# A transformer block with routed experts on one core: the third pair of routed tiles is transposed from its first fetch of rows, ahead of the first outputs

## The chip, the cores and the metric

The kernel runs on one core of a Trainium2 chip. The metric is device time in microseconds of one execution; lower is better. All numbers are float32 unless a listing says otherwise.

## The reference, cut to what matters

Sixteen batches of 512 rows with 256 columns are normalised. To the input are added a linear attention and a two-level mixture of experts. In the latter each row has one hidden vector h of 512 that all experts share; two of eight experts, both of one group of four, multiply it with their own matrix, weighted by the router.

```python
xn = _layernorm(x, axis=-1)
# attention: q, k = elu(.)+1 of projections, kv = sum over rows of k v^T per head
out = (q @ kv) / max(q . sum(k), eps) @ Wo + bo
# mixture: shared part, and two routed experts for each row
shared = _swiglu(flat @ w_in.T) @ w_out.T
h = _swiglu(flat @ w1.T)
for e in range(NUM_EXPERTS):
    routed = routed + h * w_se[:, e:e + 1] @ w2[e].T
x = x + attention + shared + routed
```

## The kernel before, in words

The first part of the kernel loops over the 16 batches. For each it normalises, projects q and k, routes, and computes the hidden rows h (function `hidden_rows`, which stores them to a DRAM table `h_d`, columns 0 to 511). Function `gather` then sums the shared expert and the attention in PSUM, adds them to the residual `res`, and stores that with the two router weights to the same rows of `h_d` (columns 512 to 769). So a row of `h_d` holds all that the routed part needs: h, the base to add to, and two weights. The h columns of the last batch are in the table before `gather` of the last batch runs; the base columns of that batch only after it.

Function `order` sorts all 8192 rows by their pair of experts (twelve pairs are possible) into tiles of 128 rows, each tile with one pair. At least 67 tiles are worked on (`SURE`); more only if the counts ask for it. The lists `source` and `goal` tell which rows a tile takes and where its results go.

The second part loops over pairs of tiles (class `Tiles`, two tiles each; the last has one). Each pair goes through three steps:

- `rows()` (line 654): GpSimd issues one indirect DMA for each of the two tiles, which gathers 128 rows of `h_d` into one of four buffers, in turn `kk_all`, `qq_all`, `xn_all` and `hs_all`. These are buffers of the first part that are free by then; `hs_all` is free only when `gather` of the last batch has read it.
- `turn()` turns h into the stationary operand `hT`, in blocks of 32 by 32. ScalarE copies three of four quadrants of rows to other partitions (line 673, tile `hb`, twelve copies), VectorE transposes the first quadrant straight from the fetched rows (line 680, four instructions) and the others from `hb` (line 686, three instructions). `hT` has two buffers (tag xnT), `hb` two (tag blocks).
- `sums()` (lines 703 to 716): TensorE multiplies each tile with the matrices of its two experts (line 703, eight matmul instructions a tile), VectorE weights and adds the halves to the base (lines 710 and 713, tile `y`), and GpSimd stores the rows to the output with an indirect DMA (line 716).

The order of issue on each engine is the order of the program as the scheduler arranges it, unless a line asks for another (`tc.issue_after`). On GpSimd all fetches and all stores of the routed part are in one queue. `AHEAD` is 3: at the change of the two parts, the first three pairs are fetched before `gather` of the last batch, so that their h is at hand early; the first two are turned right after `gather`, VectorE's part behind the last two additions of line 535 (list `taken`). Then the fourth pair is fetched, and the first three are fetched once more, because their base columns may belong to the last batch:

```python
    tiles[AHEAD].rows()
    for w in tiles[:AHEAD]:
        w.rows()
```

In the loop that follows, the pair g+3 is fetched, the pair g+2 is turned and the pair g is summed. So before the change the third pair is turned in the loop's first pass, that is from the second fetch. Buffers of the fetched rows come round after four pairs, those of `hT` after two.

Of the kernel before, what the change touches and what calls it, by code (L numbers as in the profile page):

```python
# [12 lines left out]
ALU = mybir.AluOpType  # L13
# [8 lines left out]
def block_kernel(  # L22
# [29 lines left out]
    nc = tc.nc  # L52
    B, S, D = x.shape
# [23 lines left out]
    AHEAD = 3  # L77
# [21 lines left out]
    def load_x(b, pieces=1):  # L99
        xt = xp.tile([P, NT, D], FP, tag="x", name=f"x_{b}")  # L100
        n = NT // pieces
        for i in range(pieces):
            nc.sync.dma_start(
                out=xt[:, ts(i, n), :], in_=x[b, ts(i, n * P), :].rearrange("(t p) d -> p t d", p=P)
            )
        return xt
# [61 lines left out]
    def load_expert(i):  # L168
        W = HID // NQ
        for q in range(NQ):  # L170
            tc.keep_in_program_order(nc.sync.dma_start(
                out=w2_sb[ts(q, Q), :, ts(i, D)],
                in_=w2[ts(q, W), i // NL * EG + LINE[i % NL], :].rearrange("(c j) d -> j c d", j=Q),
            ))
# [57 lines left out]
    def turn(to, rows, tag, b, parts):  # L232

        blocks = work.tile([P, S // Q, KD * Q], FP, tag="blocks", name=f"{tag}_{b}")
        for q in range(NQ):
            nc.sync.dma_start(
                out=blocks[ts(q, Q)],
                in_=rows[:, ts(q, KD * Q)].rearrange("(n j) m -> j n m", j=Q),
            )

        def place():
            return nc.vector.transpose(  # L242
                to.rearrange("p c (n j) -> p n c j", j=Q),
                blocks.rearrange(f"p n {parts} -> p n c i", i=Q),
            )

        return place
# [205 lines left out]
    def key_sum(b, kk):  # L453

        k2 = one.tile([P, 2, D], FP, tag="k2", name=f"k2_{b}")
        nc.gpsimd.tensor_tensor(k2, kk[:, 0:2, :], kk[:, 2:4, :], ALU.add)  # L456
        nc.gpsimd.tensor_tensor(k2[:, 0, :], k2[:, 0, :], k2[:, 1, :], ALU.add)
        pks = ps_mm.tile([P, D], FP, tag="mm", name=f"pks_{b}")
        nc.tensor.matmul(pks, lhsT=ones, rhs=k2[:, 0, :], start=True, stop=True)  # L459
        ksb = work.tile([P, D], FP, tag="ksb", name=f"ksb_{b}")  # L460
        nc.vector.tensor_copy(ksb, pks)
        return ksb

    def summarize(b, xn, kk):

        pxk = ps_mm.tile([P, KD, D], FP, tag="mm", name=f"pxk_{b}")
        for c in range(KD):
            for t in range(NT):
                nc.tensor.matmul(  # L469
                    pxk[:, c, :], lhsT=xn[:, t, ts(c, P)], rhs=kk[:, t, :],  # L470
                    start=(t == 0), stop=(t == NT - 1),
                )
        xk = one.tile([P, KD, D], FP, tag="xk", name=f"xk_{b}")
        nc.scalar.copy(xk, pxk)
        return xk
# [166 lines left out]
    class Tiles:  # L642
# [17 lines left out]
        def turn(self, after=None):  # L660

            n, W = self.n, HID // NQ
            self.hT = work.tile([P, KH, 2 * P], FP, tag="xnT", name=f"hT_{self.tiles[0]}")
            to = self.hT.rearrange("p c (n a j) -> p n c a j", n=2, a=NQ)[:, 0:n]
            near = 1
            there = work.tile([P, NQ - near, 2, W], FP, tag="blocks", name=f"hb_{self.tiles[0]}")  # L670
            for a in range(near, NQ):
                for q in range(NQ):
                    nc.scalar.copy(  # L673
                        there[ts(q, Q), a - near, 0:n, :], self.hg[ts(a, Q), 0:n, ts(q, W)]
                    )
            wait = (lambda: tc.issue_after(after.ins)) if after else nullcontext
            for a in range(near):
                for q in range(NQ):
                    with wait():
                        nc.vector.transpose(  # L680
                            to[ts(q, Q), :, :, a, :],
                            self.hg[ts(a, Q), 0:n, ts(q, W)].rearrange("p n (c i) -> p n c i", i=Q),
                        )
            for a in range(near, NQ):
                with wait():
                    nc.vector.transpose(  # L686
                        to[:, :, :, a, :],
                        there[:, a - near, 0:n, :].rearrange("p n (c i) -> p n c i", i=Q),
                    )
            return self  # L690

        def sums(self):

            for j, i in enumerate(self.tiles):
                if i % TR == 0:
                    _, regs[:] = nc.values_load_multi_w_load_instructions(
                        self.where[i // TR : i // TR + 1, :], engines=[mybir.EngineType.PE],
                        min_val=0, max_val=(G * NL - 2) * D,
                        skip_runtime_bounds_check_because="a sum of steps up to one of the pairs, whatever the counts",
                    )  # L700
                py = ps_mm.tile([P, 2, D], FP, tag="mm", name=f"py_{i}")
                for f in range(KH):
                    nc.tensor.matmul(  # L703
                        py.rearrange("p j d -> p (j d)"), lhsT=self.hT[:, f, ts(j, P)],
                        rhs=w2_sb[:, f, bass.ds(regs[i % TR], 2 * D)],
                        start=(f == 0), stop=(f == KH - 1),
                    )
                base = self.hg[:, j, HID:ROW]
                y = work.tile([P, D], FP, tag="y", name=f"y_{i}", bufs=4)
                nc.vector.scalar_tensor_tensor(  # L710
                    y, py[:, 0, :], base[:, D : D + 1], base[:, 0:D], ALU.mult, ALU.add
                )
                nc.vector.scalar_tensor_tensor(  # L713
                    y, py[:, 1, :], base[:, D + 1 : D + 2], y, ALU.mult, ALU.add
                )
                stored = nc.gpsimd.indirect_dma_start(  # L716
                    out=out_rows,
                    out_offset=bass.IndirectOffsetOnAxis(ap=self.goal[:, i : i + 1], axis=0),
                    in_=y, in_offset=None, bounds_check=TT * P - 1, oob_is_err=False,
                )  # L720

                tc.declare_no_dep(stored.ins, group="out", reason="no two tiles write to the same row")
                tc.add_to_no_dep_group("out", stored.ins)

    def front(b, xnT):

        res = residual(b)
        qq, kk, lg = project(b, xnT)
        route(b, lg, res)
        return res, qq, kk  # L730
# [8 lines left out]
    for b in range(B):  # L739
        xn, xnT, _ = normed.pop(b)  # L740
        res, qq, kk = fronts.pop(b)
        if b + 1 < B:
            fronts[b + 1] = front(b + 1, normed[b + 1][1])
        else:

            nc.sync.dma_start(
                out=h_d[ts(b, S), HID:ROW].rearrange("(t p) h -> p t h", p=P), in_=res
            )
            *lists, filled = order()
            tiles = [Tiles(list(range(i, min(i + 2, SURE))), *lists) for i in range(0, SURE, 2)]  # L750
        xk = summarize(b, xn, kk)
        if b == 0:
            sums = key_sum(0, kk)
            queries[0] = attend(0, qq, sums)
        if b + 2 < B:
            normed[b + 2] = normalize(b + 2)
        if b + 3 < B:
            xs[b + 3] = load_x(b + 3)
        hidden_rows(b, xnT)
        ksb, (qT, turned) = sums, queries.pop(b)  # L760
        turned()
        if b + 1 < B:
            sums = key_sum(b + 1, fronts[b + 1][2])
            queries[b + 1] = attend(b + 1, fronts[b + 1][1], sums)
        hs = hidden(b, xnT)
        kvo = mix(b, xk, ksb)
        if b + 2 < B:
            normed[b + 2][2]()
        if b + 1 == B:
            for w in tiles[:AHEAD]:  # L770
                w.rows()
        taken = gather(b, res, qT, kvo, hs)
        if b + 1 == B:

            tiles[0].turn(taken[-2])
            tiles[1].turn(taken[-1])

        for e in waiting[: 2 if b + 1 < B else G * NL]:
            load_expert(e)
        waiting = waiting[2:]  # L780
# [8 lines left out]
    for g, w in enumerate(tiles):  # L789
        if 0 < g < len(tiles) - AHEAD:  # L790
            tiles[g + AHEAD].rows()
        if g + AHEAD - 1 < len(tiles):
            tiles[g + AHEAD - 1].turn()
        w.sums()

    def rest(i):
        if i < TILES:
# [44 lines left out]
```

## Time and profile before

| | |
|---|---|
| median of three runs | 1091.64 us (1086.5, 1091.64, 1130.06) |
| the profiled execution | 1087.99 us |
| its span | 1086.2 us |
| TensorE busy | 1055.5 us (97%) |
| VectorE busy | 660.9 us (61%) |
| ScalarE busy | 375.9 us (35%) |
| GpSimd busy | 243.9 us (22%) |
| mean granted TensorE clock | 0.993 |

The span is the time from the first to the last instruction that the profiler saw in one execution. A row of the profile's groups gives line, engine, operation, output and input, the count, then the busy time in us and the mean in ns, and after the second bar the idle time of the engine ahead of it and what ended that. In a timeline the columns are start, duration (both in us), engine, line, operation and count, and in brackets the idle time ahead and what ended it. The clock row shows the TensorE clock granted, in tenths of full speed.

### The profile page before, as it was taken

The page shows a single profiled execution, that of the slowest core. Times are in us where ns is not written, and L with a number is a line of the kernel's source. Part 1 is how long each engine was busy: PE and PEld are TensorE (multiplying, and loading weights), DVE is VectorE, ACT ScalarE, POOL GpSimd, SP SyncE. Part 2 cuts the span into 40 slices and gives each one's busy share as a digit, 9 for nine tenths or more (in the row PEclk, how much of TensorE's full clock was granted, in tenths as well). Part 3 has the DMA queues.
Part 4 walks back from the last instruction along what each step waited for, and adds up shares of the span by engine and source line. Part 5 has one row for each costly group of instructions (what it writes and reads, how often), then busy time and mean ns, then how long its engine had stood idle before and what let it go on. Part 6 is the DMA issues. An engine that isn't in the chain of part 4 may idle for free.

```text
span 1086.2 us, 11307 instructions
## 1 busy us (share of the span) xinstructions
PE 1055.5 (97%) x3404; PEld 627.5 (58%) x3404; DVE 660.9 (61%) x1744; ACT 375.9 (35%) x703; POOL 243.9 (22%) x313
## 2 busy tenths in 40 slices
PE   6999999999999999999999999999999699999996
PEld 5574747575666657574747575666646244444442
DVE  7947466564647474746556464647395466666663
ACT  3413232223223131313222232212013667777761
POOL 6102011020202020101101020202003555555552
PEclk9999999999999999999999999999999899999999
DMA  7243342433424243423131323221114544555540
GB/s 228 97 117 117 78 135 59 135 92 105 133 69 136 69 136 88 125 59 115 41 116 57 100 72 91 81 63 63 59 40 133 185 136 152 150 151 152 153 151 34
DMA packets 129054, 116.02 MB, mean 107 GB/s; under 512 B 72109, under 2 KB 113597, under 8 KB 128736
## 3 DMA queue, kind: packets, MB, share of 16 engines
q1 hardware_dynamic: 119120, 77.16, 23.7%
q0 software_dynamic: 9456, 37.59, 11.4%
q8 instruction: 29, 0.48, 0.2%
q10 hardware_dynamic: 416, 0.52, 0.1%
q14 instruction: 33, 0.27, 0.1%
HBM read 65.36 MB, written 50.27 MB: 106 GB/s over the span
## 4 chain that ended last, share of the span: by engine, by line
PE 94%; DVE 2%; DMA 1%; issue 1%; ACT 0%; POOL 0%; SPq 0%; POOLq 0%; DVEq 0%; ACTq 0%
PE py L703 21%; PE phr L424 20%; PE phs L443 20%; PE po L534 15%; PE pxk L469 5%; PE pk L312 5%; PE pq L323 5%; PE pm L499 2%; PE pvk L482 1%; PE pks L459 1%; DMA x<-in_x 0%; DMA xn_all<-h_d,source 0%; ACT hb L673 0%; DMA hs_all<-h_d,source 0%; PE pi L614 0%
## 5 line engine op out<-in xcount | busy, mean ns | idle before, releaser
L703 PE MATMUL py<-w_sb,hT 128*128 x536 | 233.5, 599 | 10.0 <-DVE hT L686 10.0
L443 PE MATMUL phs<-xnT,win_sb 128*128 128x512 f32 x512 | 223.6, 593 | 0.0
L424 PE MATMUL phr<-w_sb,xnT 128*128 128x512 f32 x512 | 222.8, 593 | 0.0
L703 PEld LDWEIGHTS py<-w_sb,hT 128*128 128x128 f32 x536 | 103.0, 193 | 140.0 <-issue 138.9
L424 PEld LDWEIGHTS phr<-w_sb,xnT 128*128 128x128 f32 x512 | 97.3, 190 | 114.5 <-issue 106.0
L443 PEld LDWEIGHTS phs<-xnT,win_sb 128*128 128x128 f32 x512 | 97.0, 190 | 113.0 <-issue 110.3
L292 POOL TENSOR_TENSOR res<-x,bo_sb 128x1024 f32<-128x1024 f32 x16 | 37.9, 2369 | 433.9 <-DMA h_d<-res 323.4
L534 PE MATMUL po<-wout_sb,hs_all 128*128 128x256 f32 x512 | 123.6, 380 | 0.0
L535 DVE TENSOR_TENSOR res<-po,res 128x256 f32<-128x256 f32 x64 | 27.2, 424 | 131.8 <-PE po L534 131.8
L534 PEld LDWEIGHTS po<-wout_sb,hs_all 128*128 128x128 f32 x512 | 96.3, 191 | 12.2
L450 DVE TENSOR_TENSOR hs_all<-phs,sa_hs 128x512 f32<-128x512 f32 x64 | 43.5, 680 | 90.7 <-PE phs L443 85.4
L449 ACT ACTIVATE sa_hs<-phs 128x512 f32<-128x512 f32 x64 | 38.2, 597 | 158.4 <-PE phs L443 153.3
L716 POOL DMA_INDIRECT out<-y,goal x67 | 67.6, 1009 | 88.4 <-DVE y L713 78.0
L301 ACT ACTIVATE km<-km 128x1024 f32<-128x1024 f32 x16 | 16.9, 1057 | 177.4 <-DVE km L300 177.4
L432 DVE TENSOR_TENSOR hr<-phr,sa_hr 128x512 f32<-128x512 f32 x64 | 43.8, 684 | 55.7 <-PE phr L424 32.8
L430 ACT ACTIVATE sa_hr<-phr 128x512 f32<-128x512 f32 x64 | 38.0, 597 | 99.2 <-PE phr L424 93.3
L534 PE MATMUL po<-kvo,qT 128*128 128x256 f32 x256 | 67.0, 384 | 0.0
L312 PE MATMUL pk<-wkr_sb,xnT 128*128 128x266 f32 x256 | 61.3, 393 | 2.0 <-DVE xnT L242 1.7
L469 PE MATMUL pxk<-kk_all,xn_all 128*128 128x256 f32 x256 | 58.0, 380 | 0.0
L323 PE MATMUL pq<-wq_sb,xnT 128*128 128x256 f32 x256 | 57.9, 379 | 0.0
L456 POOL TENSOR_TENSOR k<-kk_all 128x512 f32<-128x512 f32 x16 | 27.6, 1727 | 127.8 <-DVE sm L358 125.3
L312 PEld LDWEIGHTS pk<-wkr_sb,xnT 128*128 128x128 f32 x256 | 49.1, 193 | 11.3 <-DVE xnT L242 2.1
(148 smaller groups left out, 1261.5 us busy)
## 6 DMA issues: line engine op xcount, KB each, us to landing
h_d<-hr SPq DMA_DIRECT2D x64, 256.0 KB, 2.6
h_d<-res SPq DMA_DIRECT2D x64, 129.0 KB, 1.9
q_d<-qq_all SPq DMA_DIRECT2D x16, 512.0 KB, 2.8
qb<-q_d SPq DMA_DIRECT2D x64, 128.0 KB, 2.6
w_sb<-in_w SPq DMA_DIRECT2D x64, 128.0 KB, 3.5
x<-in_x SPq DMA_DIRECT2D x15, 512.0 KB, 4.3
xn_d<-xn_all SPq DMA_DIRECT2D x14, 512.0 KB, 3.0
xb<-xn_d SPq DMA_DIRECT2D x56, 128.0 KB, 3.3
```

The source lines that it names most:

```text
L312: nc.tensor.matmul(pk, lhsT=xnT[:, k, ts(t, P)], rhs=wkr_sb[:, k, :], start=(k == 0), stop=(k == KD - 1),)
L323: nc.tensor.matmul(pq[:, t, :], lhsT=xnT[:, k, ts(t2 + t, P)], rhs=wq_sb[:, k, :], start=(k == 0), stop=(k == KD - 1),)
L424: nc.tensor.matmul(ph, lhsT=xnT[:, k, ts(t, P)], rhs=w1_sb[:, k, ts(half, HID)], start=(k == 0), stop=(k == KD - 1),)
L430: nc.scalar.activation(sa, halves[0], AF.Silu)
L432: nc.vector.tensor_tensor(hr, halves[1], sa, ALU.mult)
L443: nc.tensor.matmul(ph, lhsT=win_sb[:, k, ts(half * KH + f, P)], rhs=xnT[:, k, :], start=(k == 0), stop=(k == KD - 1),)
L449: nc.scalar.activation(sa, halves[0], AF.Silu)
L450: nc.vector.tensor_tensor(h[:, f, :], halves[1], sa, ALU.mult)
L469: nc.tensor.matmul(pxk[:, c, :], lhsT=xn[:, t, ts(c, P)], rhs=kk[:, t, :], start=(t == 0), stop=(t == NT - 1),)
L534: nc.tensor.matmul(po, lhsT=a, rhs=w, start=(i == 0), stop=(i == len(parts) - 1))
L703: nc.tensor.matmul(py.rearrange("p j d -> p (j d)"), lhsT=self.hT[:, f, ts(j, P)], rhs=w2_sb[:, f, bass.ds(regs[i % TR], 2 * D)], start=(f ...
L716: stored = nc.gpsimd.indirect_dma_start(out=out_rows, out_offset=bass.IndirectOffsetOnAxis(ap=self.goal[:, i : i + 1], axis=0), in_=y, in_ ...
```

## The change

The third pair (`tiles[2]`) is turned where the first two are, after `gather` of the last batch and ahead of the second fetch, from the rows of its first fetch. `turn()` keeps its last transpose in `self.turned`. The first pass of the loop no longer turns a pair; the later passes turn the same pairs as before. In the first pass `sums()` is given that transpose, and VectorE's first addition of each of the two first tiles is issued only behind it.

```diff
             for a in range(near, NQ):
                 with wait():
-                    nc.vector.transpose(
+                    self.turned = nc.vector.transpose(
                         to[:, :, :, a, :],
                         there[:, a - near, 0:n, :].rearrange("p n (c i) -> p n c i", i=Q),
                     )
             return self
 
-        def sums(self):
+        def sums(self, after=None):
...
-                nc.vector.scalar_tensor_tensor(
-                    y, py[:, 0, :], base[:, D : D + 1], base[:, 0:D], ALU.mult, ALU.add
-                )
+                with tc.issue_after(after.ins) if after else nullcontext():
+                    nc.vector.scalar_tensor_tensor(
+                        y, py[:, 0, :], base[:, D : D + 1], base[:, 0:D], ALU.mult, ALU.add
+                    )
...
             tiles[0].turn(taken[-2])
-            tiles[1].turn(taken[-1])
+            for w in tiles[1:AHEAD]:
+                w.turn(taken[-1])
...
-        if g + AHEAD - 1 < len(tiles):
+        if 0 < g < len(tiles) - AHEAD + 1:
             tiles[g + AHEAD - 1].turn()
-        w.sums()
+
+        w.sums(tiles[AHEAD - 1].turned if g == 0 else None)
```

## The prediction

> **What bounds the kernel now.** I read the page first: the busy shares, the two rows of tenths for PE and its clock, and the row of the routed matmuls.
>
> ```profile
> span 1086.2 us, 11307 instructions
> PE 1055.5 (97%) x3404; PEld 627.5 (58%) x3404; DVE 660.9 (61%) x1744; ACT 375.9 (35%) x703; POOL 243.9 (22%) x313
> ...
> PEclk9999999999999999999999999999999899999999
> ...
> L703 PE MATMUL py<-w_sb,hT 128*128 x536 | 233.5, 599 | 10.0 <-DVE hT L686 10.0
> ```
>
> TensorE is busy for 97% of the span, so only its gaps can be won. One slice of its clock row shows 8 instead of 9, and the routed matmuls of line 703 waited 10.0 us for transposes of line 686. PE's waits say how that splits.
>
> ```profile
> PE py L703 <- DVE hT L686: 10.0, 2, 9.2
> PE pt L280 <- DVE xn_all L270: 8.5, 2, 8.2
> ```
>
> Two waits for hT, one of 9.2 us (the columns are total, times, longest); the second row belongs to the start of the program. PE's timeline places the long one: after 32 matmuls, which are two pairs of routed tiles (4 tiles of 8), and ahead of the third pair.
>
> ```profile
> 833.45 14.00 PE L703 MATMUL py<-w_sb,hT 128*128 x32 [0.75 <-DVE hT L686]
> 856.69 23.76 PE L703 MATMUL py<-w_sb,hT 128*128 x48 [9.24 <-DVE hT L686]
> ```
>
> Next the windows, first of the stretch itself (the columns are PE, PEld, DVE, ACT and POOL busy, then clock, DMA share and GB/s), then of line 703 alone, pair by pair.
>
> ```profile
> 847.45:856.69 9.24, 0.00 (x1) 0.03 (x1) 5.81 (x14) 5.40 (x14) 5.75 (x6) 0.76 0.74 227
> 856.69:862.69 6.00, 6.00 (x7) 2.50 (x8) 1.56 (x4) 5.80 (x15) 1.99 (x2) 0.51 0.35 111
> ```
>
> ```profile
> 833.45:840.30 6.85, 6.85 (x16) 3.15 (x17) 1.00 0.40 124
> 856.69:866.60 9.91, 9.91 (x17) 4.26 (x18) 0.70 0.25 81
> 866.60:873.47 6.87, 6.87 (x18) 3.05 (x17) 1.00 0.25 76
> ```
>
> The gap costs twice. The third pair runs at clock 0.51 for its first 6.0 us and takes 9.91 us where the others take 6.86. What it waited for is seen on three queues. GpSimd's:
>
> ```profile
> 827.74 0.95 POOL L654 DMA_INDIRECT xn_all<-h_d,source  x1 [0.30 <-issue]
> 837.16 0.95 POOL L654 DMA_INDIRECT hs_all<-h_d,source  x1 [8.47 <-PE py L703]
> ...
> 845.96 0.95 POOL L654 DMA_INDIRECT xn_all<-h_d,source  x1 [0.30 <-issue]
> 847.22 1.03 POOL L716 DMA_INDIRECT out<-y,goal  x1 [0.30 <-issue]
> ...
> 851.14 0.98 POOL L654 DMA_INDIRECT kk_all<-h_d,source  x1 [0.30 <-issue]
> ```
>
> ScalarE's:
>
> ```profile
> 832.36 4.97 ACT L673 COPY hb<-qq_all 32x256 f32<-32x256 f32 x12
> 851.10 4.97 ACT L673 COPY hb<-xn_all 32x256 f32<-32x256 f32 x12 [13.76 <-DMA xn_all<-h_d,source]
> ```
>
> VectorE's:
>
> ```profile
> 837.37 0.45 DVE L686 STREAM_TRANSPOSE hT<-hb 128x256 f32<-128x256 f32 x1 [1.18 <-ACT hb L673]
> 844.42 0.48 DVE L710 SCALAR_TENSOR_TENSOR y<-py,kk_all 128x256 f32<-128x256 f32 x1 [6.61 <-DMA kk_all<-h_d,source]
> ...
> 850.77 1.78 DVE L680 STREAM_TRANSPOSE hT<-xn_all 32x256 f32<-32x256 f32 x4 [2.82 <-DMA xn_all<-h_d,source]
> ...
> 856.10 0.45 DVE L686 STREAM_TRANSPOSE hT<-hb 128x256 f32<-128x256 f32 x1 [0.24 <-ACT hb L673]
> ```
>
> The third pair's rows lie in xn_all. They are fetched twice. The second round starts at 837.16, and its fetch into xn_all, the last of eight, landed at 850.75 (issued at 845.96, 4.8 us to landing). Only then did ScalarE, idle for 13.76 us, copy and VectorE transpose. Yet the first fetch of the same rows was issued by 827.74, takes at most 4.7 us, so lay there from 832.4 on, unused.
>
> [...] The trace agrees on the halving (0.51) but gives other times: it fell about 4.9 us after the last matmul and came back 6.0 us after the next. I use the 6.0 us. [...] here 0.95 us against 3.7 to 4.9 us to landing, so I count landings. [...]
>
> **The change, part by part.** No instruction is added or removed: 12 copies, 7 transposes and all DMAs stay. They are recorded earlier, and GpSimd keeps its order.
>
> *ScalarE's copies for pair 3.* They follow those of pair 2, which end at 837.33 (832.36 + 4.97): data there since 832.4, the buffer of pair 1's copies free since 833.4. They run 837.33 to 842.30, in idle time.
>
> *VectorE's seven transposes.* hT has two buffers, so the third waits for pair 1's matmuls: 833.45 + 6.86 = 840.3, with the drain 840.5. Four of 0.44 us (1.77), then three of line 686 (1.10): done at about 843.5, in the idle 6.61 us. PE needs it at 833.45 + 2 x 6.86 = 847.2: slack 3.7 us. The gap of 9.24 us goes, and the half-clock stretch with it: 9.91 - 6.86 = 3.05 us. Together 12.3 us.
>
> *The added wait.* Both first outputs of line 711 wait for the last transpose (843.5), but kk_all's second fetch lands at 844.4 anyway. Price nothing, cover 0.9 us. Behind them queue y of the first pair, GpSimd's stores and the fetches of pair 5 (kk_all).
>
> *GpSimd's new wait.* The second fetch into xn_all must now wait for the last read of the first one, ScalarE's at 842.30 and VectorE's at 842.3. Its slot is 844.70: nothing, cover 2.4 us. SP's queue is not touched: its last stores are out by 834.2.
>
> *What is late next.* Pair 4 (hs_all) landed by 842.8; copies 842.8 to 847.8, transposes from 847.9 (behind y of the third tile) to 850.8; needed at 847.2 + 6.86 = 854.0: no wait. Pair 5 is the next: its fetch keeps its slot at 851.14 and took 4.9 us, landing at 856.0. Before, nobody needed it then (its matmuls started at about 873.4). Now ScalarE starts 0.35 us later as at 851.10, copies until 861.4, one transpose of 0.45 us more, and PE starts 0.14 us after that: 862.0, while PE comes free at 854.0 + 6.86 = 860.9. A new wait of 1.1 us. Were the landing as quick as in the later stream (3.9 us), it would be 0.1; with another microsecond of congestion, 2.1. I take 1.1; all stay under the 4.9 us at which the clock fell. Pair 6: copies 861.4 to 866.4, transposed at 866.9, needed at 862.0 + 6.86 = 868.9. Pair 7: its second fetch waits for the store of y behind pair 5's transposes, 864.3, landing 868.3, ready at about 874.1 against 875.7. After that the slack grows to the steady stream's 4 us, and the tail of 10.0 us after the last matmul stays.
>
> Sum: 9.24 + 3.05 - 1.1 = 11.2 us. The profiled execution took 1087.99 us (its span 1086.2 and 1.8 around it): 1087.99 - 11.2 = 1076.8. The median of the runs shown, 1091.64, stands 3.7 above that execution, the lowest at 1086.5. I say 1077.0, on the profiled execution's footing; on the median's it would be 1080.4, inside the range.
>
> **The rivals.**
>
> *A, as worked out: 1077.0.*
>
> *B, the wait moves to pair 5.* Late fetches, busier than in the trace of before (0.88 DMA share between 840 and 850), arrive some 4 us later: a gap of 5 us, in which the clock falls too, 3 us more. Gain 12.3 - 8 = 4.3: 1083.7. For it: 1.1 us are missing already. Against: up to 851 the traffic and its order are the same.
>
> *C, the clock stays low though the gap is gone.* Then 9.24 - 1.1 = 8.1: 1079.9. Against: it was 1.00 in all windows without a gap.
>
> *D, slower.* The new waits form a loop of queues: GpSimd's xn_all fetch stands ahead of the first stores and the fetches of pair 5, and is held until the third pair was read. If it issues late by d past 844.70, pair 5 is late by 1.1 + d, and 3 us of low clock join in. The gain of 12.3 is used up at d = 8.2, when the third pair's reads end after 852.9. With d = 12 it is slower by 3.8: 1091.8. For it: every fetch is in one queue. Against: copies and transposes have all their data ten microseconds before.
>
> *E, the change doesn't do what it says.* If the transposes still hung on the second fetch, the outputs would wait with them: about 1088. Against: the compiled order has the xn_all copies wait on the DMA semaphores of the first fetch, and its second fetch wait on ScalarE.
>
> **How the numbers follow.** A 0.77, B 0.10, C 0.05, D 0.04, E 0.04. The range, 1073 to 1085.5, takes A's 1075.8 to 1077.9 for the unknown landing, B and C, and the 3.7 us between execution and median. Two per cent, about what a measurement of this kernel can tell from no change, is 22 us; all of hT's waiting and the slow stretch are 13. Faster by over 2%: 0.02; within: 0.95; slower: 0.03, D grown or a disturbed measurement.
>
> **What would show it.** In the profile after: PE's longest wait for hT at about 1 us ahead of pair 5; clock 1.00 throughout 840 to 870; ScalarE's copies from xn_all starting at 837.3 without idling; VectorE's first output still at about 844.4, ended by kk_all's DMA. The first output at 848 or later would speak for D, a gap over 4 us before pair 5 for B, a span above 1082 against A.

## The result, and the profile after

The changed kernel took 1077.47 us (median of 6 runs, 1075.93 to 1079.28), the kernel before 1089.85 us (median of 6, 1085.69 to 1130.06). The ratio is 0.9897, with a 95% interval of 0.9873 to 0.9921, so the gain of 1.0% is clear of the noise, though small, and it is where the prediction put it. The ratio leaves out the execution of 1130.06 us, which is 4% above the fastest of its kernel. The profiled execution took 1076.49 us.

One thing is needed to read the times of all kernels here. Four of the eleven profiles shown or summed up below, one of them of the changed kernel, have a further wait of TensorE of 3.6 to 4.5 us near the start (it begins at 18.55, 18.57 and 18.73 us in three of them). The changed kernel's third profile shows half clock with it, 0.50 from 21.4 to 28.2 us; in two others the 16 matmuls of line 312 behind it take 5.2 and 5.3 us, where the 16 ahead of it took 4.8 and 4.9. It is far from the change. In these four and in the kernel with 8 more copies the first routed matmul starts at 837.0 to 838.9 us, in the others at 832.3 to 833.5, so it costs about 5 us. Each run has one kept profile, so that this wait also explains why the times of one kernel spread over some 5 us is likely, but not shown. What compares kernels best is therefore the routed stretch of the profiles, from the first matmul of line 703 to the last.

The page of the changed kernel (its lines behind the changed one are numbered one higher, so line 710 is now 711 and line 716 is 717):

```profile
span 1074.8 us, 11307 instructions
PE 1052.6 (98%) x3404; PEld 624.7 (58%) x3404; DVE 661.1 (62%) x1744; ACT 375.9 (35%) x703; POOL 244.9 (23%) x313
...
PEclk9999999999999999999999999999999999999999
...
L703 PE MATMUL py<-w_sb,hT 128*128 x536 | 230.5, 592 | 2.0 <-DVE hT L686 2.0
```

The counts of instructions are those of before. The clock row has no 8 any more, the routed matmuls are 3.0 us shorter in sum (230.5 for 233.5), and their wait for hT is 2.0 us for 10.0. PE's timeline shows what is left:

```profile
832.61 27.73 PE L703 MATMUL py<-w_sb,hT 128*128 x64 [0.75 <-DVE hT L686]
861.64 28.56 PE L703 MATMUL py<-w_sb,hT 128*128 x66 [1.29 <-DVE hT L686]
```

Four pairs run through where two did, and a new wait of 1.29 us stands ahead of the fifth. The windows of line 703 for pair 3 and pair 5 (PE, PEld, clock, DMA share, GB/s) put both at full clock:

```profile
846.33:853.20 6.87, 6.87 (x17) 3.04 (x16) 1.00 0.74 254
861.64:868.50 6.86, 6.86 (x16) 3.12 (x17) 1.00 0.48 149
```

The three queues behind it. ScalarE's timeline:

```profile
836.46 4.97 ACT L673 COPY hb<-xn_all 32x256 f32<-32x256 f32 x12
...
856.05 4.97 ACT L673 COPY hb<-kk_all 32x256 f32<-32x256 f32 x12 [7.62 <-DMA kk_all<-h_d,source]
```

VectorE's:

```profile
839.78 1.78 DVE L680 STREAM_TRANSPOSE hT<-xn_all 32x256 f32<-32x256 f32 x4 [2.87 <-PE py L703]
841.60 1.10 DVE L686 STREAM_TRANSPOSE hT<-hb 128x256 f32<-128x256 f32 x3
844.57 0.48 DVE L711 SCALAR_TENSOR_TENSOR y<-py,kk_all 128x256 f32<-128x256 f32 x1 [1.87 <-DMA kk_all<-h_d,source]
...
861.05 0.45 DVE L686 STREAM_TRANSPOSE hT<-hb 128x256 f32<-128x256 f32 x1 [1.22 <-ACT hb L673]
```

GpSimd's:

```profile
845.01 0.94 POOL L654 DMA_INDIRECT xn_all<-h_d,source  x1 [0.30 <-issue]
...
847.51 1.04 POOL L717 DMA_INDIRECT out<-y,goal  x1 [0.30 <-DVE y L711]
...
851.45 0.98 POOL L654 DMA_INDIRECT kk_all<-h_d,source  x1 [0.30 <-issue]
```

ScalarE copies the third pair without idling, its transposes end at 842.7 (841.60 + 1.10), and VectorE's first output (the addition of line 711) comes 1.87 us after that, when kk_all's fetch has landed: so the transposes lie in what had been idle time. GpSimd's second fetch into xn_all did not wait for the new reader (0.30 us ahead of it, ended by nothing but issue). The fetch of pair 5, issued at 851.45, lands at 856.0; copies to 861.0, the last transpose to 861.5, PE at 861.64. That chain is the new wait.

The routed stretch lasted 833.45 to 1076.16, 242.7 us, in the kernel before, and 832.61 to 1064.46, 231.85 us, in the changed one: 10.86 us less. Removed were 9.24 (gap) and 3.05 (half clock), added 1.29: 11.0. Of the 11.4 us between the two spans, another 0.84 lies ahead of the stretch, at the start of the program, and is no work of the change; the tail grew by 0.3.

### The profile page after: what moved, and what is told of

Its sections match the earlier page's. It is cut to its first block, busy times and chain, and to the rows that moved or that the text cites. A ratio compares the mean times of both kernels' runs of the same rounds, so it can differ in the third digit from the quotient of the medians.

```text
span 1074.8 us, 11307 instructions
## 1 busy us (share of the span) xinstructions
PE 1052.6 (98%) x3404; PEld 624.7 (58%) x3404; DVE 661.1 (62%) x1744; ACT 375.9 (35%) x703; POOL 244.9 (23%) x313
## 3 DMA queue, kind: packets, MB, share of 16 engines
q0 software_dynamic: 9456, 37.59, 11.4%
## 4 chain that ended last, share of the span: by engine, by line
PE 91%; DVE 4%; DMA 2%; issue 1%; ACT 1%; POOL 1%; SPq 0%; POOLq 0%; ACTq 0%; DVEq 0%
PE phs L443 20%; PE py L703 20%; PE phr L424 19%; PE po L534 15%; PE pk L312 5%; PE pxk L469 5%; PE pq L323 5%; PE pm L499 1%; PE pvk L482 1%; DMA kk_all<-h_d,source 1%; PE pks L459 1%; ACT hb L673 1%; DMA xn_all<-h_d,source 0%; DMA x<-in_x 0%; DVE qm L300 0%
## 5 line engine op out<-in xcount | busy, mean ns | idle before, releaser
L703 PE MATMUL py<-w_sb,hT 128*128 x536 | 230.5, 592 | 2.0 <-DVE hT L686 2.0
```

Source lines behind the costliest of these rows:

```text
L703: nc.tensor.matmul(py.rearrange("p j d -> p (j d)"), lhsT=self.hT[:, f, ts(j, P)], rhs=w2_sb[:, f, bass.ds(regs[i % TR], 2 * D)], start=(f ...
```

## The experiments

A sum is used in all of them. Take the changed kernel's stretch without its wait: 231.85 - 1.29 = 230.55 us. To it are added a kernel's waits for hT within the stretch and half of the TensorE time under half clock (0.50 to 0.51 in the windows). The third column is that sum, the last is measured from the first to the last routed matmul of each profile.

| kernel | waits; work at half clock (us) | sum | measured |
|---|---|---|---|
| before | 9.24; 5.9 | 242.7 | 242.7 |
| before, gap filled with matmuls | 8.75 of filler, 1.90; none | 241.2 | 241.0 |
| changed | 1.29; none | 231.85 | 231.85 |
| changed, without the order on the outputs | 2.02, 0.17; none | 232.7 | 233.0 |
| changed, another round of fetches, first time | 5.98; 6.2 | 239.6 | 239.6 |
| the same, second time | 0.52; none | 231.1 | 231.2 |
| changed, second time | 6.06; 3.2 | 238.2 | 238.2 |
| changed, third time | 1.25; none | 231.8 | 231.8 |
| changed, fourth time | 0.52; none | 231.1 | 231.1 |
| changed, 8 more copies | 1.55; none | 232.1 | 232.1 |
| changed, 24 more copies | 5.79, 0.81; 3.1 | 238.7 | 238.9 |

Sum and measurement agree within 0.3 us. So nothing else moves in the stretch: a kernel's time there is its waits and its clock. The experiments were run on three occasions, each on another chip. To the first belong the filled gap, the kernel without the order, the other round of fetches for the first time and the changed kernel for the second; to the next the changed kernel for the third time and both kernels with more copies; to the last the other round for the second time and the changed kernel for the fourth.

### Is the slow third pair a result of the gap? The gap filled with matmuls

The kernel before, with ten matmuls of 512 columns (20 instructions) on a spare PSUM tile behind the second pair. They add work that nobody reads.

```diff
-                    nc.tensor.matmul(
+                    self.last = nc.tensor.matmul(
...
         w.sums()
+        if g == 1:
+            fill = ps_y.tile([P, 2 * D], FP, tag="py", name="fill")
+            for f in range(10):
+                with tc.issue_after(w.last.ins):
+                    nc.tensor.matmul(
+                        fill, lhsT=w2_sb[:, f % KH, 0:P], rhs=w2_sb[:, f % KH, 0 : 2 * D],
+                        start=True, stop=True,
+                    )
```

> The kernel before, with ten extra matmuls of 128x512 (20 instructions, about 8.6 us at 0.43 us each) on TensorE between the second and the third pair; their result is not used. Nothing else moves: the third pair still starts when its transposes are done, some 23.2 us after the first routed matmul. Theory (the slow stretch is a consequence of TensorE's idling): the clock stays at 1.00, the third pair takes 6.9 us instead of 9.9, and the time is 3 us below the kernel before, about 1086.8 against its 1089.85 median (1085.0 against its profiled 1087.99). Rival (the slow stretch belongs to the transfers and transposes of those microseconds): the third pair still takes 9.9 us and the time stays that of the kernel before.

Measured: 1085.92 us (median of 22) beside 1088.37 for the kernel before (30), ratio 0.9982, interval 0.9968 to 0.9996. PE's timeline and the window of pair 3 (all engines, then clock, DMA share and GB/s):

```profile
851.00 8.75 PE L799 MATMUL fill<-w_sb 128*128 128x512 f32 x20
861.64 38.86 PE L703 MATMUL py<-w_sb,hT 128*128 x90 [1.90 <-DVE hT L686]
```

```profile
861.64:868.50 6.86, 6.86 (x16) 3.12 (x17) 2.41 (x6) 6.62 (x17) 2.80 (x3) 1.00 0.34 112
```

With 1.90 us of idle time instead of 9.24 the third pair takes 6.86 us at clock 1.00, though its rows still come from the second fetch. The half-clock stretch was the gap's own second cost, and it goes with the gap; the rival in which it stays has nothing left. The gain in time, 0.18%, is 2.4 us between the medians; the profile gives the 3.05 of the stretch less 1.4 by which pair 3 was later on that occasion (8.75 + 1.90 against 9.24).

### What does the order on the outputs bring? The changed kernel without it

```diff
-        w.sums(tiles[AHEAD - 1].turned if g == 0 else None)
+        w.sums()
```

> The changed kernel without its ordering edge: the first output is not issued behind the third pair's transposes. On VectorE the first tile's two additions then stand in front of these transposes, the second tile's behind them; on GpSimd the first fetch of the fifth pair moves ahead of the second fetch into xn_all. Theory (VectorE serves in order, and an addition that waits for kk_all's second fetch holds the transposes): the transposes start after the first output at about 845.5, the third pair is ready at 848.4 instead of 842.7, TensorE waits 2.2 us ahead of it and about 0.6 us ahead of the fifth pair instead of 1.3; the time is 1.5 us above the changed kernel, about 1079. Rival (the edge is idle, the early fetch alone brings the gain): no wait ahead of the third pair, and the same time as the changed kernel, 1077.5.

Measured: 1079.55 us (median of 6), ratio 0.9908, interval 0.9886 to 0.9929. PE's timeline of pairs 1 to 5, and VectorE's at the first outputs:

```profile
837.04 14.00 PE L703 MATMUL py<-w_sb,hT 128*128 x32 [0.74 <-DVE hT L686]
853.07 13.97 PE L703 MATMUL py<-w_sb,hT 128*128 x32 [2.02 <-DVE hT L686]
867.21 33.28 PE L703 MATMUL py<-w_sb,hT 128*128 x77 [0.17 <-DVE hT L686]
```

```profile
849.10 0.48 DVE L711 SCALAR_TENSOR_TENSOR y<-py,kk_all 128x256 f32<-128x256 f32 x1 [7.54 <-DMA kk_all<-h_d,source]
...
850.02 1.77 DVE L680 STREAM_TRANSPOSE hT<-xn_all 32x256 f32<-32x256 f32 x4
```

The first output takes VectorE's place and waits 7.54 us for kk_all's second fetch; the transposes of pair 3, whose buffer of hT was free from 843.9 on (837.04 + 6.86), stand behind it and begin at 850.02. Yet it costs only 2.02 us, and pair 5's wait falls to 0.17. The fetch that pair 5 waits for last did not come earlier: it was issued at 856.84, 19.80 us after the first routed matmul, for 18.84 in the changed kernel. TensorE itself was 2 us later, so this wait hides in the one ahead of pair 3. Turning pair 3 from its first fetch thus brings nearly all of the gain. What the order on the outputs brings is less sure. Against the first profile of the changed kernel it is 2.02 + 0.17 - 1.29 = 0.9 us. But on the occasion of this run the changed kernel took 1082.83 us, longer in each of its six runs than this one in any of its six, which fits the wait of 6 us that its profile has there (the next experiment shows it). So no run shows that the kernel with the order is the faster one.

### Is pair 5's wait that of its fetch? Another second round, twice, and the changed kernel beside it

The second round fetches the first pair, then the fourth, then the second; the third pair's second fetch goes behind pair 5's fetches.

```diff
-                nc.gpsimd.indirect_dma_start(
+                self.got = nc.gpsimd.indirect_dma_start(
...
-    tiles[AHEAD].rows()
-    for w in tiles[:AHEAD]:
+    for w in (tiles[0], tiles[AHEAD], tiles[1]):
         w.rows()
...
+        if g == 1:
+            with tc.issue_after(tiles[g + AHEAD].got.ins):
+                tiles[AHEAD - 1].rows()
```

> The changed kernel with GpSimd's second round of fetches in another order: kk_all ahead of hs_all, and the second fetch into xn_all behind the two fetches of the fifth pair. The same fetches and bytes. Theory (the fifth pair's wait of 1.29 us comes from its place in GpSimd's queue): the first outputs come 2 us earlier, the fifth pair's second fetch is issued at about 849.0 instead of 851.45 and lands at about 853.4, its transposes are done at 859.2 where TensorE comes free at 860.2; the wait of 1.29 us goes and no other comes; the time is 1.2 us below the changed kernel, about 1076.2. Rival (the wait comes from crowded transfers, which take the longer the closer they follow each other): the fetch lands at 855 or later and the wait stays near 1 us.

> The changed kernel once more, beside the others on the same chip. All theories: 1077.5 within 1.5 us; TensorE waits about 1.3 us ahead of the fifth pair and not ahead of the third, and the clock is 1.00 through the routed stretch.

Measured: 1083.54 us (median of 9, 1081.51 to 1086.12), ratio 0.9947, interval 0.9928 to 0.9966, and for the changed kernel beside it 1082.83 (median of 6, 1081.84 to 1083.64), ratio 0.9942, interval 0.9923 to 0.9961. They are 7.3 and 5.3 us above what the theory gave. The reordered kernel, ScalarE's timeline, VectorE's and PE's at pair 5:

```profile
853.50 4.98 ACT L673 COPY hb<-kk_all 32x256 f32<-32x256 f32 x12 [2.83 <-DMA kk_all<-h_d,source]
```

```profile
862.93 1.78 DVE L680 STREAM_TRANSPOSE hT<-kk_all 32x256 f32<-32x256 f32 x4 [7.17 <-remote]
```

```profile
865.98 19.19 PE L703 MATMUL py<-w_sb,hT 128*128 x37 [5.99 <-DVE hT L686]
```

The fetch came some 3 us earlier, as wanted: it was issued at 848.87, ScalarE's wait for it ended at 853.5, not at 855 or later as with the crowded transfers of the rival, and copies were done at 858.5. But VectorE began its transposes at 862.93 only ("remote" stands for a wait whose end the profile could not put down to an instruction or a transfer). The changed kernel on that occasion, the same three engines:

```profile
856.64 5.00 ACT L673 COPY hb<-kk_all 32x256 f32<-32x256 f32 x12 [7.87 <-issue]
```

```profile
856.88 0.48 DVE L711 SCALAR_TENSOR_TENSOR y<-py,xn_all 128x256 f32<-128x256 f32 x1 [4.25 <-PE py L703]
...
863.29 1.78 DVE L680 STREAM_TRANSPOSE hT<-kk_all 32x256 f32<-32x256 f32 x4 [5.40 <-remote]
```

```profile
866.34 3.97 PE L703 MATMUL py<-w_sb,hT 128*128 x5 [6.06 <-DVE hT L686]
```

Here too the rows were in time. What was late, as far as the records go, is VectorE's start behind TensorE: this output's matmuls ended, by the records, at 849.98, and it began at 856.88; the buffer of hT that the transposes need was last read at 853.4, and they began at 863.29. The profile puts 4.25 us of the first delay down to TensorE, and 5.40 us of the second to nothing that it could name. TensorE meanwhile went on through pairs 3 and 4 without a pause, so a delay of 7 to 10 us between the two is what the records show. That TensorE's signals came late is the author's reading of it, and no run here shows the cause. The kernel without the order, on the same occasion, had no such wait (2.02 us was its longest). A wait of 6 us ahead of pair 5 let the clock fall (0.50 from 862.7 to 869.5), which is rival B's outcome by another way than B's.

Both were run once more on a later occasion.

> The reordered second round (kk_all's rows first, xn_all's second fetch behind those of pair 5) measured once more, because on the first occasion VectorE saw TensorE's signals late and pair 5 waited 6 us for that alone. Theory: the wait ahead of pair 5 is that of its fetch; with the fetch issued some 2.5 to 3 us earlier it is gone (below 0.4 us), and the time is 1 to 1.3 us below that of the changed kernel on the same occasion, near 1076. Rival: pair 5 is bound by VectorE's queue and TensorE's signals, not by its fetch; a wait of 1 us or more (up to 6) stays ahead of it and the time is that of the changed kernel or longer.

> The changed kernel beside the reordered one. Theory: 1077, with a wait of 1.2 to 1.5 us ahead of pair 5, ended by ScalarE's copies of kk_all, which wait for its fetch. Rival, where TensorE's signals are seen late again: a wait of 6 us ahead of pair 5 with kk_all already landed and copied, and 1082.

Measured: 1075.68 us (median of 6), ratio 0.989, interval 0.9872 to 0.9907, for the reordered kernel, and 1076.55 us (median of 5), ratio 0.9895, interval 0.988 to 0.991, for the changed one. PE's timelines, first of the reordered kernel, then of the changed one:

```profile
837.36 34.72 PE L703 MATMUL py<-w_sb,hT 128*128 x80 [0.75 <-DVE hT L686]
872.60 27.70 PE L703 MATMUL py<-w_sb,hT 128*128 x64 [0.52 <-DVE hT L686]
```

```profile
832.62 27.73 PE L703 MATMUL py<-w_sb,hT 128*128 x64 [0.74 <-DVE hT L686]
860.88 39.29 PE L703 MATMUL py<-w_sb,hT 128*128 x91 [0.52 <-DVE hT L686]
```

VectorE did not start late behind TensorE this time. In the reordered kernel five pairs run through and the wait of 0.52 us stands ahead of pair 6, whose fetch had become the last; that no other wait would come was wrong. In the changed kernel it stands ahead of pair 5, where 1.2 to 1.5 us were expected, and again its fetch ends it, through ScalarE's copies:

```profile
855.28 4.97 ACT L673 COPY hb<-kk_all 32x256 f32<-32x256 f32 x12 [7.30 <-DMA kk_all<-h_d,source]
```

Counted from the first routed matmul these copies start at 22.66 us and the wait is 0.52 us; on the first occasion they start at 23.44 and the wait is 1.29. The copies moved by 0.78 and the wait by 0.77. So it is the fetch that binds there, as predicted, but moving one fetch forward moves another back: the stretches measure 231.2 and 231.1 us. The medians differ by 0.9 us with intervals that overlap nearly whole, so the reordered kernel is not shown to be better.

### Does the gain come again? The changed kernel on a third occasion

> The changed kernel a third time, on another occasion. On the second occasion TensorE waited 6.06 us ahead of the fifth pair instead of 1.29, because VectorE's instructions that wait for TensorE's matmuls (the addition for the fifth tile, the first transposes of the fifth pair) started 6 to 10 us after these matmuls had ended, with all their transfers landed. Theory (TensorE's signals come late on some occasions, whatever the kernel's transfers): either about 1077.5 with a wait of 1.3 us, or about 1082.5 with a wait of about 6 us, all runs of the occasion alike. Rival (the fifth pair's transfers are late): the wait follows the landing of the fetch, and ScalarE's copies from it start late as well.

Measured: 1081.38 us (median of 5, 1075.84 to 1082.62), ratio 0.991, interval 0.9876 to 0.9943. PE's timeline at pair 5 has the small wait again:

```profile
867.89 27.28 PE L703 MATMUL py<-w_sb,hT 128*128 x63 [1.25 <-DVE hT L686]
```

The copies for pair 5 start 23.39 us after the first routed matmul (862.29 - 838.90), which fits the wait as above. The higher time does not come from the routed stretch, which measured 231.8 us: this profile, of an execution of 1082.62 us, has the wait near the start, 4.45 us at 18.55, with half clock after it. So 6 us ahead of pair 5 belong to one occasion, and 0.5 to 1.3 us to the three others. The chip differed too, so the runs do not tell whether it is the occasion or the chip. On all four the changed kernel was faster than the kernel before, by ratios of 0.9897, 0.9942, 0.991 and 0.9895.

### How much slack has pair 3? More copies on ScalarE

In front of the third pair's copies ScalarE makes 8 (3.4 us) or 24 (10.2 us) more, of rows that are then written over by the right ones. This delays exactly what rival D delays: the end of the reads of xn_all.

```diff
             there = work.tile([P, NQ - near, 2, W], FP, tag="blocks", name=f"hb_{self.tiles[0]}")
+            if self.tiles[0] == 2 * (AHEAD - 1):
+                for i in range(8):
+                    nc.scalar.copy(
+                        there[ts(i % NQ, Q), 0, 0:n, :], self.hg[ts(near, Q), 0:n, ts(i % NQ, W)]
+                    )
```

(The numbers of the later lines grow by 5.) With 8:

> The changed kernel with eight extra copies on ScalarE ahead of the third pair's copies, 3.3 us (they write what is overwritten). Theory (3.7 us of slack on the third pair, cover for both new waits): the copies end at about 844.7, the transposes at 845.2, TensorE needs them at 846.3; the second fetch into xn_all keeps its slot at 845.0; no wait ahead of the third pair, the first output 0.7 us later, the time that of the changed kernel on the same chip within 1 us. Rival (the new waits already decide): every microsecond of the delay is seen, the time rises by about 3 us.

Measured: 1080.69 us (median of 6, 1076.02 to 1083.42), ratio 0.9906, interval 0.9876 to 0.9935; the changed kernel on that occasion took 1081.38. PE's timeline, and GpSimd's at xn_all's second fetch:

```profile
837.32 27.73 PE L708 MATMUL py<-w_sb,hT 128*128 x64 [0.75 <-DVE hT L691]
866.60 28.56 PE L708 MATMUL py<-w_sb,hT 128*128 x66 [1.55 <-DVE hT L691]
```

```profile
849.92 0.95 POOL L654 DMA_INDIRECT xn_all<-h_d,source  x1 [1.92 <-ACT hb L678]
```

No wait ahead of pair 3. Its transposes end 2.7 us later than in the changed kernel, counted from the first routed matmul (850.13 - 837.32 for 842.70 - 832.61), and TensorE needs them 0.9 us after that: 3.6 us of slack in all, for 3.7 predicted. That xn_all's second fetch keeps its slot, as was expected too, did not come true: GpSimd stood idle for 1.92 us ahead of it, until ScalarE had read xn_all, for 0.30 without the extra copies. Even so, pair 5's wait is only 0.3 us longer than in the changed kernel. With 24:

> The changed kernel with 24 extra copies on ScalarE ahead of the third pair's copies, 10 us. The third pair's reads then end at 851.4, its transposes at 851.9; TensorE waits about 5.7 us ahead of it, with or without a fall of the clock (3 us); GpSimd's second fetch into xn_all is held from 845.0 to 851.5, and with it the first stores and the fifth pair's fetches. By the prediction's rival D (the loop of queues adds its wait at the fifth pair): a further wait of 1.3 + 6.5 us there, in all some 11 us above the changed kernel, about the time of the kernel before. By the theory that one wait hides the other (TensorE is late itself when the fifth pair is needed): 0 to 2.5 us ahead of the fifth pair, in all 7 us above the changed kernel on the same chip.

Measured: 1085.79 us (median of 13, 1083.01 to 1088.88), ratio 0.9967, interval 0.9947 to 0.9986. GpSimd's timeline, PE's, and a window of the half clock:

```profile
851.77 0.94 POOL L654 DMA_INDIRECT xn_all<-h_d,source  x1 [8.12 <-ACT hb L678]
```

```profile
852.13 15.50 PE L708 MATMUL py<-w_sb,hT 128*128 x32 [5.79 <-DVE hT L691]
868.44 11.83 PE L708 MATMUL py<-w_sb,hT 128*128 x27 [0.81 <-DVE hT L691]
```

```profile
848.40:855.20 6.80, 3.07 (x4) 1.51 (x5) 4.31 (x11) 6.56 (x17) 2.82 (x3) 0.50 0.24 61
```

This is rival D with its full delay: the fetch issues 19.44 us after the first routed matmul (851.77 - 832.33), where the prediction's slot was 844.70 - 833.45 = 11.25, so d is 8.2, exactly where D had the gain used up. It was not. The wait shows at pair 3 itself (5.79 us), the two pairs after it take 1.5 us more, part of them at half clock (15.50 for 14.00), and pair 5's wait is smaller than before, 0.81. By the table the stretch is 7.1 us longer than the changed kernel's, where D's working gave 11.2. (The medians of that occasion differ by only 4.4 us; the wait near the start is in the changed kernel's profile there and not in this one.) Counted from the first routed matmul, pair 5's fetch is issued 7.0 us later than in the changed kernel (25.87 for 18.84), and TensorE comes free for that pair 7.6 us later (35.30 for 27.74): one wait hides in the other, and D had put the whole delay at pair 5.

## Why the prediction was right

The mechanism held, and so did the two large terms: 1077.0 against a median of 1077.47, and 1076.8 against 1076.49 for the profiled execution. That the median agrees so closely is in part luck. The number stood on the footing of one profiled execution; on that of the medians the prediction had 1080.4, and on the later occasions the changed kernel took 1082.83, 1081.38 and 1076.55 us. Step by step:

- *The gap and the half clock.* Both terms went whole, 9.24 and 3.05. The filled gap shows that the half clock follows from the idle time (1.00 behind an idle 1.90 us, 0.51 behind 9.24).
- *ScalarE's copies of pair 3* were put at 837.33 to 842.30; they ran 836.46 to 841.4, all 0.8 us earlier, as the whole stretch began 0.84 us earlier. They did not idle.
- *VectorE's transposes and the first outputs.* Counted from the first routed matmul the transposes were done at 10.1 us, as predicted (842.70 - 832.61 and 843.5 - 833.45); they began 0.31 us after the first pair's matmuls by the windows (839.47 to 839.78), where the prediction's drain was 0.2. The cover of 0.9 us was really 1.87, because kk_all's rows came 1.0 us later, not because VectorE was faster. With the 8 added copies the first output came another 0.8 us later, and pair 5's wait grew by 0.3 only.
- *GpSimd's new wait* cost nothing, as priced. In the four profiles of the changed kernel the second fetch never waited for the third pair's reads (0.30 us ahead of it in each).
- *Pair 5's new wait* was put at 1.1 us, with 0.1 to 2.1 as ends; it was 1.29, 1.25 and 0.52 on three occasions. The fourth, of 6.06, had another reason. In the first the right size is luck, since errors nearly cancel. Counted from the first routed matmul, the fetch was issued 1.15 us later than assumed (18.84 for 17.69), since the last store of `res` landed 3.8 us after its issue for 2.6 and the second round waits for it. The step "its fetch keeps its slot" was thus wrong. Against this the fetch landed in 4.5 us for 4.9, ScalarE began 0.1 us after the landing for 0.35, and TensorE came free for pair 5 at a time 0.3 us later than assumed.
- *The first outputs' added order* was not priced as a gain. Between two profiles of different occasions it is 0.9 us; the times measured side by side do not show it.
- *Rival B* (a gap of 5 us moves to pair 5, with low clock) was seen in the changed kernel on one occasion, at 6.06 us, though not by congestion of fetches: the rows had landed. The prediction had no term for a late start of VectorE behind TensorE.
- *Rival C* falls with the clock of 1.00 at pairs 3 and 5, *rival E* with ScalarE's copies at 836.46. *Rival D* fails in its price: the sum "1.1 + d, and 3" counts the wait at pair 5 in full though the same delay has by then been paid at pair 3. At d = 8.2 the kernel was still faster (0.9967); taking every further microsecond as one microsecond of wait, an estimate from the measured 7.1 and the gain of 11, the break-even lies near d = 12. That was not tried.
- *The range* of 1073 to 1085.5 was wider than this result needed, which lies in A's own 1075.8 to 1077.9. The medians of two later occasions do need it. The prediction also took 2% as about what a measurement can tell from no change; the intervals here reach 0.1 to 0.3% to either side, and the change of 1% stands out of them. The source of the 3.7 us between execution and median, most likely the wait near the start, was not known then.

## What to carry to other kernels

A gap of TensorE was worth its length here (9.24 us) and, as the clock fell in it, half of the time that TensorE then worked at half clock (3.05 us), so one row of the wait list can hide a second cost in the windows. When a wait goes, follow each queue to the next arrival that has no slack: here 1.29 us of 12.3 came back at pair 5, and moving that fetch forward only passed a wait of 0.52 us to pair 6. Delays in one chain didn't add where one wait covered the other (7.1 us with 24 added copies, where the sum was 11.2); price the second from when the first ends.

## What the runs showed of the hardware

The half-clock stretches of the routed part lasted 10.2 us at the gap before (0.50 from 852.3 to 862.5) and 6.8 us in three others: with 24 added copies (0.50 from 848.4 to 855.2), in the changed kernel's second time (862.7 to 869.5) and in the reordered kernel's first (865.3 to 872.1). After the wait near the start it was 6.8 us in the changed kernel's third time (21.4 to 28.2). Behind the last routed matmul the clock is low too, 0.74 in the mean from 1064.6 to 1074.8 in the changed kernel, and there the profile ends.

How long TensorE idled before the clock fell differs: 4.9 us after the last matmul in the kernel before (847.45 to 852.3) and 5.3 us in the reordered kernel's first time (859.99 to 865.3), but 2.1 us with 24 added copies (846.33 to 848.4) and 2.4 us in the changed kernel's second time (860.28 to 862.7). It didn't fall in the idle 0.5 to 2.0 us of the other waits in the routed part (1.00 through the 1.90 us behind the filled gap and after it). So "under 4.9 us" was no safe bound in the prediction; by the recorded ends of the matmuls, no run here shows a fall after less than 2.1.

The wait near the start and VectorE's late starts behind TensorE stay without a cause: they stand in some profiles of the changed kernel and not in others.
